# Two batches together in the stationary operand: both convolutions of a conv-plus-scores kernel with 64x128 weights on halves of the PE array, in place of 64x64 weights on quarters

## The chip, the cores and the metric

The kernel runs on one core of one Trainium2 chip. The metric is the device time of one execution in microseconds (us). Three runs of the kernel before took 876.03, 878.07 and 881.8 us; the median is 878.07 us. The profile is of one execution with a span of 872.5 us from its first to its last instruction, on core 0, the only one used.

In what follows PE is the matrix engine (TensorE), PEld its weight loads, DVE VectorE, ACT ScalarE, POOL GpSimd and SP SyncE, which issues most of the DMAs.

## The reference, cut to what matters

Input x is (4, 64, 256, 256) float32: 4 batches, 64 channels, images of 256x256. Layer 0 convolves each channel's image with a 256x256 kernel that is an outer product of two vectors of 256, made by two small sine networks from `z`, and adds `x * bias`. Layer 1 forms, for each batch and channel, the Gram matrix of the image's rows, weighs it, sums each row of it, adds that sum to the row and normalises each channel over batch and image.

```python
# layer 0
k = jnp.einsum('ijk,imk->ijmk', hx, hy)[0]           # outer product for each channel
y = irfft2(rfft2(x, 512) * rfft2(k, 512) / 512)[..., :256, :256]
x = y + x * bias[:, None, None]
# layer 1
scores = jnp.einsum('bpsd,bptd->bpst', x, x) * inv_dim
red = jnp.sum(scores * weights[None], axis=-1, keepdims=True)
y = x + red
mean, var = jnp.mean(y, (0, 2, 3)), jnp.var(y, (0, 2, 3))     # keepdims
out = (y - mean) * lax.rsqrt(var + 1e-5) * gamma + beta
```

As the kernel of layer 0 is an outer product, the 2-D convolution is one along the columns followed by one along the rows, and each is a product with a lower triangular Toeplitz matrix. All arithmetic is float32.

## The kernel before

The kernel takes the 64 channels one after the other. For a channel c the 4 batches are written as two bits (u, v), and 256 rows or columns as 4 blocks of 64. PE has three stages for a channel:

- `conv_z(c, m)` (line 211), m = 0, 1: the convolution along the columns. Weights (`lhsT`) are 64x64 blocks of the image, moving data (`rhs`) are rows of the Toeplitz tile `toep`. A block i of 64 columns reaches only the outputs behind it, so that its moving data has 256 - 64 i columns: 256, 192, 128 and 64. The result lies in a PSUM tile p1 for each u, and `copy_z` (line 220, ACT) copies it to the tile z in SBUF with its columns turned round.
- `conv_x0(c, z)` (line 236; `first_x0`, line 265, for channel 0): the same along the rows, with 64x64 blocks of z as weights. `add_bias` (line 246, DVE) adds `bias * x` on the way from PSUM (p2) to the tile x0 in SBUF.
- `gram(c, v)` (line 299): the blocks of the Gram matrix, 64x64 weights, moving data of 192 and 128 columns. `weigh` (DVE, lines 319 and 328) multiplies with the weights and sums.

The tensor engine's array has 128 rows and 128 columns. A product of 64 rows (its contraction) by 64 columns (of its weights) takes one quarter of it. The row half is given by the partitions of the operands, the column half by the partitions of the output. In the convolutions the four products of one step, t = 0 to 3, go to the four quarters: two bits of the batch are row half and column half. In `conv_z` u is the row half and v the column half, in `conv_x0` it is the other way round.

The order on every engine is written out by hand (`manual_schedule`). In the main loop of channel c, PE runs `conv_x0(c)`, `conv_z(c + 1, 0)`, `conv_z(c + 1, 1)`, `gram(c, 0)`, `gram(c, 1)`, so that ACT's copy of z lies beside other products. SP issues the loads of x for channels c + 2 and c + 3 in four DMAs of 256 KB for a channel, among the loads of `toep`, the weights and the stores of finished channels. PSUM has 8 banks, given out in turn from one pool `ps`. Near the end, in `last_channels`, the row sums of the last three channels are made by PE in place of POOL (`red_by_pe`, lines 379 and 384, weights of 128 rows by 64 columns), and the last channel's moments too (`sum_of`, line 507, weights of 128x128 and moving data of one column). At the start two products with 128x128 weights (line 168) keep PE running while the first Toeplitz tile lands.

The x tiles before: `xts[c, v]` of shape [128, 4, 256], with partition (u, column in its block), then block of columns, then row. The tile z before: [128, 2, 4, 256], with partition (v, row in its block), then u, block of rows, column.

Of the kernel before, what the change touches and what calls it, by code (L numbers as in the profile page):

```python
# [8 lines left out]
F32 = mybir.dt.float32  # L9
AF = mybir.ActivationFunctionType  # L10
ALU = mybir.AluOpType
# [4 lines left out]
B, C, S = 4, 64, 256  # L16
P = 128
# [4 lines left out]
H = P // 2  # L22
# [15 lines left out]
def conv_scores_bn_kernel(  # L38
# [19 lines left out]
    nc = tc.nc  # L58
# [3 lines left out]
    ld = ctx.enter_context(tc.tile_pool(name="ld", bufs=3))  # L62
    wk = ctx.enter_context(tc.tile_pool(name="wk", bufs=2))
    sm = ctx.enter_context(tc.tile_pool(name="sm", bufs=3))

    xts, ws, hs = {}, {}, {}

    def load_xt(c, v, n):
        if not n:
            xts[c, v] = ld.tile([P, 4, S], F32, tag=f"xt{v}", name=f"xt_{c}_{v}", bufs=4)  # L70
        part = bass.ts(n, 2)
        nc.sync.dma_start(xts[c, v][:, part], xT[c, v, :, part])

    PARTS = ((0, 0), (1, 0), (0, 1), (1, 1))

    def load_w(c):
        w = ld.tile([P, 10, H], F32, tag="w", name=f"w_{c}", bufs=2)
        nc.sync.dma_start(w, wl[c])
        ws[c] = w
# [20 lines left out]
    nc.sync.dma_start(decay0_sb, decay0)  # L100
    decay_sb = const.tile([P, S], F32, name="decay_sb")
    nc.sync.dma_start(decay_sb, decay)
    for part in PARTS:
        load_xt(0, *part)
    eye_sb = const.tile([P, P], F32, name="eye_sb")
    nc.sync.dma_start(eye_sb, eye)
    chan_sb = const.tile([P, 3, C], F32, name="chan_sb")
    nc.sync.dma_start(chan_sb.rearrange("p a c -> p (a c)"), chan.to_broadcast([P, 3 * C]))
    load_w(0)
    for part in PARTS:  # L110
        load_xt(1, *part)
    g_sb = const.tile([P, GW], F32, name="g_sb")
    nc.vector.memset(g_sb[:, S:], 0.0)

# [8 lines left out]
    with tc.tile_pool(name="fps", bufs=4, space=PSUM) as fps:  # L123
# [3 lines left out]
        for layer in range(3):  # L127
            for n in range(2):
# [5 lines left out]
                a = wk.tile([P, P], F32, tag="fa", name=f"fa_{layer}_{n}")  # L134
# [3 lines left out]
                k = wk.tile([P, P], F32, tag="fk", name=f"fk_{layer}_{n}")  # L138
# [39 lines left out]
    def load_h(c, n):  # L178


        if not n:
            hs[c] = ld.tile([P, 2, GW], F32, tag="toep", name=f"toep_{c}")
        src = bass.AP(
            g_dram.tensor, g_dram.offset + c * 2 * GW + 16 * n,
            [[4 + C * 2 * GW, COPIES], [1, 4], [1, GW + S]],
        )
        rows = hs[c][bass.ts(n, 16)].rearrange("p a r -> p (a r)")
        nc.sync.dma_start(rows[:, : GW + S], src)

    def copy_h(c):  # L190

        toep = hs[c]
        nc.scalar.copy(toep[H:, :, :S], toep[:H, :, :S])  # L193
# [5 lines left out]
    st8, zs = {}, {}  # L199

    def conv_z(c, m):


        toep = hs[c]
        p1 = [ps.tile([P, 2, S], F32, tag="ps", name=f"p1_{c}_{m}_{u}") for u in range(2)]
        for k in range(2):
            for i in range(4):
                for t in range(4):
                    u, v = t % 2, t // 2
                    rows = bass.ts(u, H)  # L210
                    nc.tensor.matmul(  # L211
                        p1[u][bass.ts(v, H), k, : S - H * i],
                        lhsT=xts[c, v][rows, i, bass.ts(2 * m + k, H)],
                        rhs=toep[rows, 1, H * i : S], start=(i == 0), stop=(i == 3),
                    )
        return p1

    def copy_z(c, m, p1):
        for u in range(2):
            nc.scalar.copy(zs[c][:, u, bass.ts(m, 2), :], p1[u][:, :, ::-1])  # L220

    def conv_x0(c, z, parts=range(2)):


        toep = hs[c]
        if not c:
            first_x0(z)
            return
        for m in parts:
            p2 = [ps.tile([P, 2, S], F32, tag="ps", name=f"p2_{c}_{m}_{v}") for v in range(2)]  # L230
            for i in range(2):
                for k in range(4):
                    for t in range(4):
                        v, u = t % 2, t // 2
                        rows = bass.ts(v, H)
                        nc.tensor.matmul(  # L236
                            p2[v][bass.ts(u, H), i, : S - H * k],
                            lhsT=z[rows, u, k, bass.ts(2 * m + i, H)],
                            rhs=toep[rows, 0, H * k : S], start=(k == 0), stop=(k == 3),
                        )  # L240
            add_bias(c, m, p2)

    def add_bias(c, m, p2):
        for v in range(2):
            part = bass.ts(m, 2)
            nc.vector.scalar_tensor_tensor(  # L246
                st8[c][0][:, v, part], xts[c, v][:, part], chan_sb[:, 0, c : c + 1],
                p2[v][:, :, ::-1], ALU.mult, ALU.add,
            )

    def first_x0(z):

        toep = hs[0]
        p2 = [
            [ps.tile([P, 2, S], F32, tag="ps", name=f"p2_0_{m}_{v}") for v in range(2)]
            for m in range(2)
        ]
        for half in range(2):
            for m in range(2):
                for i in range(2):  # L260
                    for k in range(2 * half, 2 * half + 2):
                        for t in range(4):
                            v, u = t % 2, t // 2
                            rows = bass.ts(v, H)
                            nc.tensor.matmul(  # L265
                                p2[m][v][bass.ts(u, H), i, : S - H * k],
                                lhsT=z[rows, u, k, bass.ts(2 * m + i, H)],
                                rhs=toep[rows, 0, H * k : S],
                                start=(i == 0 and k == 0), stop=(i == 1 and k == 3),
                            )  # L270
                if half:
                    add_bias(0, m, p2[m])

    def begin(c):
        x0 = wk.tile([P, 2, 4, S], F32, tag="x0", name=f"x0_{c}", bufs=5)
        red0 = sm.tile([P, B, 2], F32, tag="red0", name=f"red0_{c}")
        sp = wk.tile([P, B, S], F32, tag="sp", name=f"sp_{c}")
        pr = wk.tile([P, B, S], F32, tag="pr", name=f"pr_{c}")
        rd = wk.tile([P, B, S], F32, tag="rd", name=f"rd_{c}")
        st8[c] = (x0, red0, sp, pr, rd)  # L280
# [129 lines left out]
    def minus_mean(mom):  # L410
        nc.scalar.activation(mom[:, 4:5], mom[:, 2:3], AF.Identity, bias=mom[:, 3:4])  # L411
        nc.scalar.activation(mom[:, 5:6], mom[:, 4:5], AF.Identity, scale=-1.0 / (B * S * S))
# [7 lines left out]
    def sum_squares(c, mom):  # L420
        tot = sm.tile([P, 3], F32, tag="tot", name=f"tot_{c}")
        nc.gpsimd.partition_all_reduce(tot[:, 0:2], mom[:, 6:8], P, RED.add)  # L422
        return tot
# [208 lines left out]

    for n in range(4):
        load_h(1, n)
    for part in PARTS:
        load_xt(2, *part)

    def begin_z(c):  # L640
        zs[c] = wk.tile([P, 2, 4, S], F32, tag="z", name=f"z_{c}")

    begin_z(0)
    for u in range(2):
# [4 lines left out]
    def parts_of(c, place):  # L649

        e, f = c - 4, c - 3
        parts = [[(e, 0, 1)], [(e, 1, 0)], [(e, 1, 1)], [(f, 0, 0)], []]
        if c >= C - 4:
            parts[4] = [(f, 0, 1)]
        if c == C - 3:
            parts[0] = []
            parts[4] += [(f, 1, 0), (f, 1, 1)]
        for i, v, n in parts[place]:
            if i >= 0:
                finish(*fins[i], v, n)  # L660

    for c in range(C - 2):
        p, q, f = c - 1, c - 2, c - 3
        begin(c)
        copy_h(c + 1)
        parts_of(c, 0)
        if c + 2 < C and c:
            load_xt(c + 2, 1, 1)
        load_h(c + 2, 0)
        conv_x0(c, zs.pop(c))  # L670
        if q >= 0:
            minus_mean(moms[q])
            squares(q, moms[q], 0)
        parts_of(c, 1)
        if c + 3 < C:
            load_xt(c + 3, 0, 0)
        load_h(c + 2, 1)
        if q >= 0:
            squares(q, moms[q], 1)
            tot = sum_squares(q, moms[q])  # L680
        if f >= 0:
            fins[f] = (f, *scale_shift(f, moms.pop(f), *scales.pop(f)))
        begin_z(c + 1)
        copy_z(c + 1, 0, conv_z(c + 1, 0))
        parts_of(c, 2)
        load_h(c + 2, 2)
        if c + 3 < C:
            load_xt(c + 3, 1, 0)
        load_w(c + 1)
        load_h(c + 2, 3)  # L690
        copy_z(c + 1, 1, conv_z(c + 1, 1))
        if p >= 0:
            pick_red(p)
        parts_of(c, 3)
        if c + 3 < C:
            load_xt(c + 3, 0, 1)
        if q >= 0:
            scales[q] = root(q, tot)
        if c == C - 3:
            copy_h(c + 2)  # L700
        parts_of(c, 4)
        gram(c, 0)
        if p >= 0:
            moms[p] = add_red(p)
        if c == BY_PE:
            all_sum(c, slice(0, 2))
        gram(c, 1)
        if c < BY_PE:
            all_sum(c)
# [72 lines left out]
```

## Time and profile before

| what | value |
|---|---|
| three runs | 876.03, 878.07, 881.8 us |
| span of the profiled execution | 872.5 us |
| median minus that span | 5.6 us |
| mean granted clock of PE over the span | 0.994 |
| records of products, and of weight loads | 24674 each |
| of these `conv_z`, `conv_x0`, `gram` | 8192, 8192 (8064 at line 236, 128 at line 265), 8192 |
| DMA, share of the 16 engines, one period | 58 to 59%, 195 to 211 GB/s |

The program has half as many products as there are records: a float32 product runs as two passes, each with its own weight load and its own record. So one `conv_z` of a channel has 64 products in the program and 128 records.

How to read it: the shares of busy time are over the span, and a record of a product covers its way through the array as well as the stretch in which it takes in columns, so that records of one quarter overlap each other. What a stage takes is therefore read from where stages begin and end, not from summed durations.

### The profile page before, as it was taken

How to read it: one execution, taken by the hardware profiler on the slowest of the kernel's cores; microseconds unless marked ns; L12 is line 12 of the kernel's file. 1: busy time of each engine (PE TensorE's matmuls, PEld its weight loads, DVE VectorE, ACT ScalarE, POOL GpSimd, SP SyncE). 2: the span in 40 equal slices, each digit the busy share in tenths (PEclk: the TensorE clock that was granted, in tenths of full speed). 3: DMA queues.
4: the chain of work that ended last, by engine and by line, in shares of the span. 5: the costliest groups of instructions: out<-in, count | busy, mean ns of one | idle time of the engine just before them, and what ended most of it. 6: DMA issues, size and time to landing. Idle time of an engine off the chain costs nothing.

```text
span 872.5 us, 55963 instructions
## 1 busy us (share of the span) xinstructions
PE 855.9 (98%) x24674; PEld 836.2 (96%) x24674; DVE 755.9 (87%) x2647; ACT 621.9 (71%) x1218; POOL 427.8 (49%) x194
## 2 busy tenths in 40 slices
PE   7999999999999999999999999999999999999995
PEld 5999999999999999999999999999999999999994
DVE  3588988988988988988998998998998988988996
ACT  2256767767767767777777777777777767767786
POOL 0236546546546546546546546546546546546530
PEclk9999999999999999999999999999999999999997
DMA  6724665565565556565565565655555655565535
GB/s 189 221 77 139 198 209 195 201 211 193 201 210 192 200 196 206 202 207 193 203 208 192 203 206 194 205 200 199 203 201 199 202 203 192 204 210 193 190 141 194
DMA packets 89870, 169.69 MB, mean 194 GB/s; under 512 B 10555, under 2 KB 11740, under 8 KB 89628
## 3 DMA queue, kind: packets, MB, share of 16 engines
q1 hardware_dynamic: 88972, 165.52, 55.6%
q8 instruction: 194, 3.18, 1.6%
q10 hardware_dynamic: 656, 0.59, 0.3%
q14 instruction: 48, 0.39, 0.2%
HBM read 98.18 MB, written 67.76 MB: 190 GB/s over the span
## 4 chain that ended last, share of the span: by engine, by line
PE 97%; DVE 2%; DMA 1%; issue 0%; ACT 0%; DVEq 0%; ACTq 0%
PE p L211 32%; PE g L299 32%; PE p L236 32%; PE p L265 0%; DMA toep<-g_sb 0%; PE ph L132 0%; DVE junk L328 0%; DMA zw_sb<-in_zw 0%; PE rp L379 0%; DVE fa L135 0%; DVE x L516 0%; DVE pr L319 0%; PE rp L384 0%; PE s L507 0%; DVE fa L140 0%
## 5 line engine op out<-in xcount | busy, mean ns | idle before, releaser
L348 POOL PARTITION_ALL_REDUCE rd<-sp x62 | 376.8, 6078 | 182.4 <-DVE sp L340 182.4
L211 PE MATMUL p<-toep,xt 64*64 64x256 f32 (+3 forms) x8192 | 304.0, 296 | 0.9 <-DMA toep<-g_sb 0.9
L299 PE MATMUL g<-x 64*64 64x192 f32 (+1 forms) x8192 | 302.5, 296 | 0.0
L211 PEld LDWEIGHTS p<-toep,xt 64*64 64x64 f32 x8192 | 291.4, 133 | 8.6 <-PE idle L168 1.5
L236 PE MATMUL p<-toep,z 64*64 64x256 f32 (+3 forms) x8064 | 298.3, 296 | 0.0
L236 PEld LDWEIGHTS p<-toep,z 64*64 64x64 f32 x8064 | 289.6, 133 | 6.8 <-issue 0.2
L299 PEld LDWEIGHTS g<-x 64*64 64x64 f32 x8192 | 289.7, 133 | 0.8 <-DVE x L246 0.2
L328 DVE SCALAR_TENSOR_TENSOR junk<-g,w 128x192 f32<-128x192 f32 x512 | 160.9, 351 | 81.1 <-PE g L299 77.7
L462 ACT ACTIVATE o<-x,sh,g 128x512 f32<-128x512 f32 x252 | 203.3, 810 | 3.0
L246 DVE SCALAR_TENSOR_TENSOR x<-xt,chan_sb,p 128x512 f32<-128x512 f32 x256 | 173.8, 739 | 7.6 <-PE p L265 7.2
L220 ACT COPY z<-p 128x512 f32<-128x512 f32 x256 | 134.7, 576 | 22.3 <-PE p L211 22.3
L416 ACT ACTIVATE sq<-x,mom 128x1024 f32<-128x1024 f32 x127 | 145.2, 1143 | 3.3 <-DVE x L405 1.1
L364 DVE SCALAR_TENSOR_TENSOR x<-x,rd 128x1024 f32<-128x1024 f32 x122 | 144.1, 1218 | 0.0
L340 DVE SCALAR_TENSOR_TENSOR sp<-eye_sb,red,pr 128x128 f32<-128x128 f32 x492 | 139.0, 344 | 0.0
L368 POOL PARTITION_ALL_REDUCE mom<-mom x61 | 24.5, 401 | 231.1 <-DVE x L364 227.1
L357 ACT COPY rd<-rd 64x512 f32<-64x512 f32 (+1 forms) x62 | 38.0, 612 | 134.8 <-POOL rd L348 134.7
L319 DVE SCALAR_TENSOR_TENSOR pr<-g,w 128x256 f32<-128x256 f32 x256 | 107.3, 419 | 0.0
L193 ACT COPY toep<-toep 64x512 f32<-64x512 f32 x63 | 38.9, 617 | 32.0 <-DMA toep<-g_dram 26.7
L411 ACT ACTIVATE mom<-mom 128x1 f32<-128x1 f32 x62 | 18.2, 293 | 38.0 <-POOL mom L368 37.1
L328 DVE DVE_READ_ACCUMULATOR junk<-g,w 128x1 f32 x512 | 42.2, 82 | 0.0
L422 POOL PARTITION_ALL_REDUCE tot<-mom x62 | 29.8, 481 | 5.1 <-ACT sq L416 5.1
L416 ACT ACTIVATION_READ_ACCUMULATOR sq<-x,mom 128x1 f32 x127 | 23.7, 186 | 0.0
(84 smaller groups left out, 220.4 us busy)
## 6 DMA issues: line engine op xcount, KB each, us to landing
xt<-in_xT SPq DMA_DIRECT2D x256, 256.0 KB
out<-o SPq DMA_DIRECT2D x256, 256.0 KB
w<-in_wl SPq DMA_DIRECT2D x64, 320.0 KB
toep<-g_dram SPq DMA_DIRECT2D x252, 36.0 KB
g_dram<-g_sb SPq DMA_DIRECT2D x1, 320.0 KB
g_dram<-g_sb ACTq DMA_DIRECT2D x1, 320.0 KB
decay_sb<-in_decay SPq DMA_DIRECT2D x1, 256.0 KB
fw_sb<-in_fw ACTq DMA_DIRECT2D x1, 192.0 KB
```

The lines of the kernel that those rows point to most:

```text
L211: nc.tensor.matmul(p1[u][bass.ts(v, H), k, : S - H * i], lhsT=xts[c, v][rows, i, bass.ts(2 * m + k, H)], rhs=toep[rows, 1, H * i : S], sta ...
L220: nc.scalar.copy(zs[c][:, u, bass.ts(m, 2), :], p1[u][:, :, ::-1])
L236: nc.tensor.matmul(p2[v][bass.ts(u, H), i, : S - H * k], lhsT=z[rows, u, k, bass.ts(2 * m + i, H)], rhs=toep[rows, 0, H * k : S], start=(k ...
L246: nc.vector.scalar_tensor_tensor(st8[c][0][:, v, part], xts[c, v][:, part], chan_sb[:, 0, c : c + 1], p2[v][:, :, ::-1], ALU.mult, ALU.add,)
L299: nc.tensor.matmul(gs[u][bass.ts(h, H), o, :], lhsT=xb[rows, v, i, m, :], rhs=xb[rows, v, i, t, :], start=(i == 0), stop=(i == 3),)
L319: nc.vector.scalar_tensor_tensor(pr[:, b].rearrange("p (t s) -> p t s", s=H), g[:, COL, :], 1.0 / math.sqrt(S), w[:, 6:10, :], ALU.mult, A ...
L328: nc.vector.scalar_tensor_tensor(junk, g[:, part, :], 1.0 / math.sqrt(S), w[:, 3 * n : 3 * n + 3, :], ALU.mult, ALU.mult, accum_out=red0[: ...
L340: nc.vector.scalar_tensor_tensor(sp[:, b, part], eye_sb, red0[:, b, n : n + 1], pr[:, b, part], ALU.mult, ALU.add,)
L348: nc.gpsimd.partition_all_reduce(rd[:, part].rearrange("p b s -> p (b s)"), sp[:, part].rearrange("p b s -> p (b s)"), P, RED.add,)
L364: nc.vector.scalar_tensor_tensor(x0[:, v], x0[:, v], 1.0, rd[:, 2 * v, None, :].to_broadcast([P, 4, S]), ALU.mult, ALU.add, accum_out=mom[ ...
L416: nc.scalar.activation(sq, st8[c][0][:, v], AF.Square, bias=mom[:, 5:6], accum_out=mom[:, 6 + v : 7 + v])
L462: nc.scalar.activation(o, y, AF.Identity, bias=sh, scale=g)
```

## The change

The products of the two column halves of one step are joined: their weights, 64x64 each, are laid side by side in SBUF and become one 64x128 operand, which gives all 128 output partitions at once. The loop over t = 0 to 3 (four quarters) becomes one over u (or v) = 0, 1 (two row halves). The number of products in both convolutions is halved, and each has the moving data it had before (256, 192, 128 or 64 columns). `gram` is not touched: it still has 64x64 weights on quarters.

So that the weights of the two batches are neighbours, x is laid out on the host as [partition (u, column), block of columns, block of rows, v, row], and z in SBUF as [partition (v, row), block of rows, block of columns, u, column]. One tile of x for a channel (`xt`, twice as large) takes the place of two, and its four DMAs are by block of columns; they are as large as before and are issued in the same places, with the same 2 KB for each partition. `copy_z` writes runs of 64 elements with gaps of 64 between them, and `add_bias` reads such runs of x; both work on as many elements as before.

```diff
-    def load_xt(c, v, n):
-        if not n:
-            xts[c, v] = ld.tile([P, 4, S], F32, tag=f"xt{v}", name=f"xt_{c}_{v}", bufs=4)
-        part = bass.ts(n, 2)
-        nc.sync.dma_start(xts[c, v][:, part], xT[c, v, :, part])
+    def load_xt(c, i):
+        if c not in xts:
+            xts[c] = ld.tile([P, 4, 4, 2, H], F32, tag="xt", name=f"xt_{c}", bufs=4)
+        nc.sync.dma_start(xts[c][:, i].rearrange("p k v s -> p (k v s)"), xT[c, :, i])
...
     def conv_z(c, m):
...
-                for t in range(4):
-                    u, v = t % 2, t // 2
+                for u in range(2):
                     rows = bass.ts(u, H)
                     nc.tensor.matmul(
-                        p1[u][bass.ts(v, H), k, : S - H * i],
-                        lhsT=xts[c, v][rows, i, bass.ts(2 * m + k, H)],
+                        p1[u][:, k, : S - H * i],
+                        lhsT=xts[c][rows, i, 2 * m + k],
                         rhs=toep[rows, 1, H * i : S], start=(i == 0), stop=(i == 3),
                     )
...
     def copy_z(c, m, p1):
         for u in range(2):
-            nc.scalar.copy(zs[c][:, u, bass.ts(m, 2), :], p1[u][:, :, ::-1])
+            nc.scalar.copy(
+                zs[c][:, bass.ts(m, 2), :, u],
+                p1[u][:, :, ::-1].rearrange("p k (b s) -> p k b s", s=H),
+            )
...
     def conv_x0(c, z, parts=range(2)):
...
-                    for t in range(4):
-                        v, u = t % 2, t // 2
+                    for v in range(2):
                         rows = bass.ts(v, H)
                         nc.tensor.matmul(
-                            p2[v][bass.ts(u, H), i, : S - H * k],
-                            lhsT=z[rows, u, k, bass.ts(2 * m + i, H)],
+                            p2[v][:, i, : S - H * k],
+                            lhsT=z[rows, k, 2 * m + i],
                             rhs=toep[rows, 0, H * k : S], start=(k == 0), stop=(k == 3),
                         )
...
     def add_bias(c, m, p2):
...
             nc.vector.scalar_tensor_tensor(
-                st8[c][0][:, v, part], xts[c, v][:, part], chan_sb[:, 0, c : c + 1],
-                p2[v][:, :, ::-1], ALU.mult, ALU.add,
+                st8[c][0][:, v, part].rearrange("p i (k s) -> p i k s", s=H),
+                xts[c][:, part, :, v], chan_sb[:, 0, c : c + 1],
+                p2[v][:, :, ::-1].rearrange("p i (k s) -> p i k s", s=H), ALU.mult, ALU.add,
             )
...
     def begin_z(c):
-        zs[c] = wk.tile([P, 2, 4, S], F32, tag="z", name=f"z_{c}")
+        zs[c] = wk.tile([P, 4, 4, 2, H], F32, tag="z", name=f"z_{c}")
...
-    xo = a["x"].reshape(2, 2, C, S, 4, H)
+    xo = a["x"].reshape(2, 2, C, 4, H, 4, H)
...
-        "xT": xo.transpose(2, 1, 0, 5, 4, 3).reshape(C, 2, P, 4, S),
+        "xT": xo.transpose(2, 0, 6, 5, 3, 1, 4).reshape(C, P, 4, 2 * S),
```

`first_x0` is changed as `conv_x0` is, and the calls of `load_xt` name a block i = 0 to 3 in place of a pair (v, n).

More of the change, by code (lines that the diff above doesn't have):

```diff
@@ L66, in conv_scores_bn_kernel @@
     xts, ws, hs = {}, {}, {}
-    def load_xt(c, v, n):
-        if not n:
-            xts[c, v] = ld.tile([P, 4, S], F32, tag=f"xt{v}", name=f"xt_{c}_{v}", bufs=4)
-        part = bass.ts(n, 2)
-        nc.sync.dma_start(xts[c, v][:, part], xT[c, v, :, part])
-    PARTS = ((0, 0), (1, 0), (0, 1), (1, 1))
+    def load_xt(c, i):
+        if c not in xts:
+            xts[c] = ld.tile([P, 4, 4, 2, H], F32, tag="xt", name=f"xt_{c}", bufs=4)
+        nc.sync.dma_start(xts[c][:, i].rearrange("p k v s -> p (k v s)"), xT[c, :, i])
     def load_w(c):
@@ L102, in conv_scores_bn_kernel @@
     nc.sync.dma_start(decay_sb, decay)
-    for part in PARTS:
-        load_xt(0, *part)
+    for i in range(4):
+        load_xt(0, i)
     eye_sb = const.tile([P, P], F32, name="eye_sb")
@@ L109, in conv_scores_bn_kernel @@
     load_w(0)
-    for part in PARTS:
-        load_xt(1, *part)
+    for i in range(4):
+        load_xt(1, i)
     g_sb = const.tile([P, GW], F32, name="g_sb")
@@ L261, in first_x0 @@
                     for k in range(2 * half, 2 * half + 2):
-                        for t in range(4):
-                            v, u = t % 2, t // 2
+                        for v in range(2):
                             rows = bass.ts(v, H)
                             nc.tensor.matmul(
-                                p2[m][v][bass.ts(u, H), i, : S - H * k],
-                                lhsT=z[rows, u, k, bass.ts(2 * m + i, H)],
+                                p2[m][v][:, i, : S - H * k],
+                                lhsT=z[rows, k, 2 * m + i],
                                 rhs=toep[rows, 0, H * k : S],
@@ L634, in conv_scores_bn_kernel @@
         load_h(1, n)
-    for part in PARTS:
-        load_xt(2, *part)
+    for i in range(4):
+        load_xt(2, i)
     def begin_z(c):
-        zs[c] = wk.tile([P, 2, 4, S], F32, tag="z", name=f"z_{c}")
+        zs[c] = wk.tile([P, 4, 4, 2, H], F32, tag="z", name=f"z_{c}")
     begin_z(0)
@@ L667, in conv_scores_bn_kernel @@
         if c + 2 < C and c:
-            load_xt(c + 2, 1, 1)
+            load_xt(c + 2, 3)
         load_h(c + 2, 0)
@@ L675, in conv_scores_bn_kernel @@
         if c + 3 < C:
-            load_xt(c + 3, 0, 0)
+            load_xt(c + 3, 0)
         load_h(c + 2, 1)
@@ L687, in conv_scores_bn_kernel @@
         if c + 3 < C:
-            load_xt(c + 3, 1, 0)
+            load_xt(c + 3, 1)
         load_w(c + 1)
@@ L695, in conv_scores_bn_kernel @@
         if c + 3 < C:
-            load_xt(c + 3, 0, 1)
+            load_xt(c + 3, 2)
         if q >= 0:
```

## The prediction

> **What bounds the kernel now.** First the head of the page, busy times and the chain that ended last:
>
> ```profile
> span 872.5 us, 55963 instructions
> PE 855.9 (98%) x24674; PEld 836.2 (96%) x24674; DVE 755.9 (87%) x2647; ACT 621.9 (71%) x1218; POOL 427.8 (49%) x194
> ...
> PE 97%; DVE 2%; DMA 1%; issue 0%; ACT 0%; DVEq 0%; ACTq 0%
> ```
>
> The end is set by PE. The question is what PE is busy with: taking in moving columns, or loading weights. PEld at 96% warns that the second is not far. The windows of one half period (two stages) and of a whole period in the steady part:
>
> ```profile
> core 0: us, PE busy (x) PEld busy (x) DVE busy (x) ACT busy (x) POOL busy (x), PEclk, DMA share, GB/s
> 404.28:408.65 4.37, 4.37 (x137) 4.27 (x133) 4.29 (x12) 4.37 (x8) 2.62 (x1) 1.00 0.59 197
> 413.08:426.16 13.08, 13.08 (x390) 12.89 (x384) 11.71 (x42) 9.73 (x20) 6.92 (x3) 1.00 0.58 197
> ```
>
> A period is 13.08 us for one channel: three stages (both convolutions and the Gram blocks) of 4.36 us. In the first row PE is in `conv_z` alone; the granted clock is full. Now the products by shape (count, busy us, mean ns of one):
>
> ```profile
> L211 PE MATMUL p<-toep,xt 64*64 64x256 f32 x2048 | 207.2, 377 | 0.9 <-DMA toep<-g_sb 0.9
> L211 PE MATMUL p<-toep,xt 64*64 64x192 f32 x2048 | 179.1, 323 | 0.0
> L211 PE MATMUL p<-toep,xt 64*64 64x128 f32 x2048 | 151.6, 269 | 0.0
> L211 PE MATMUL p<-toep,xt 64*64 64x64 f32 x2048 | 124.8, 217 | 0.0
> ```
>
> Each 64 columns more cost (377 - 217) / 3 = 53.3 ns in one pass; the rest is latency, 217 - 53 = 164 ns, in which the next record runs. So a quarter takes in a pass of 256, 192, 128, 64 columns in 213, 160, 107, 53 ns, 533 ns together. A stage has 128 records, 32 for each quarter, 8 of each width: 8 x 533 ns = 4.27 us. The stage takes 4.36 us; the 0.09 us left are about 3 ns for each of 32 records. So all four quarters stream all the time, and what is loaded is hidden entirely, even behind the narrowest products. The records of single products agree: at 851.42 us, where the quarters are in step, four 64-column products start within 20 ns and the second passes of the same four 56 ns after them.
>
> Last, what a load costs by its columns: the loads in the tail, where 128x128 weights meet one moving column, so that nothing but loading is left.
>
> ```profile
> L211 PEld LDWEIGHTS p<-toep,xt 64*64 64x64 f32 x8192 | 291.4, 133 | 8.6 <-PE idle L168 1.5
> L507 PEld LDWEIGHTS d<-last,each 128*128 128x128 f32 x2 | 0.3, 188 | 2.7 <-DVE x L516 2.7
> 863.68 0.97 PEld L507 LDWEIGHTS s<-last,each 128*128 128x128 f32 x4
> 863.20:864.50 1.30, 1.30 (x8) 1.30 (x7) 0.72 (x4) 1.30 (x2) 0.00 (x0) 0.50 0.00 0
> ```
>
> At full clock a record of 128 columns takes 188 ns against 133 ns for 64: 55 ns for 64 columns. Four loads in a row span 0.97 us at clock 0.50 (fourth row), and one of them lasts 333 ns there; they follow each other by (970 - 333) / 3 = 212 ns, 106 ns at full clock. So a load occupies its part of the array for 106 ns at 128 columns, and by the difference for about 53 ns at 64; the other 80 ns of its record are latency. A 64-column load has the length of a 64-column pass, which is why it hides today.
>
> **The change, part by part.** The sum is made against the profiled execution: 872.5 us span, and 5.6 us between it and the median of the runs.
>
> 1. *Streaming: 0.* Half as many products, each over twice the output columns, two at a time in place of four. Each row half sees 32 records in a stage, as each quarter did, with the same widths. Fewer instructions save nothing, as issue is not the bound: the four products above started 7 ns apart.
>
> 2. *Loads of 128 columns: +54.6 us.* The next load begins some 2 ns after a pass begins (single records), and is hidden if it is done when the pass has been taken in. 256 and 192 columns (213 and 160 ns) cover 106 ns; 128 columns just do (107 ns). 64 columns take 53 ns: the next pass waits 53 ns more. There are 8 such records for each half in a stage: 8 x 53.3 = 0.427 us. Two convolutions of 64 channels make 128 stages: 54.6 us. If the 128-column records lose the 3 ns of slack as well, 128 x 8 x 3 ns = 3 us come on top.
>
> 3. *Changes of the array's division: +21.9 us.* Today all three stages use quarters, and products of one stage start before the last of the other end. With the change `gram` stays on quarters, and each channel goes to halves and back. The trace has no change from 64x64 to 64x128, but the last channels go from 64x64 to 128x64 and back (the chain of waits: start, us, what):
>
> ```profile
> 839.04 0.44 PE rp L384 x8
> 839.48 2.33 PE g L299 x64
> 841.81 2.18 PE p L211 x64
> 843.99 2.18 PE g L299 x64
> 846.17 0.58 PE rp L379 x4
> ```
>
> A half `gram` after such a change takes 2.33 us, one without it 2.18: 0.15 us. The other way, four passes of 256 columns on two column halves need 2 x 216 = 0.43 us and take 0.58: again 0.15. In it lies one 53 ns load that nothing hides; towards halves this load has 128 columns, so 0.20. There are 63 changes in each direction that are new (62 rounds of the main loop and one around the last `conv_z`): 63 x (0.20 + 0.147) = 21.9 us. As both forms keep 64 rows, the price could be nothing; I take 0.147 because the rows that change form in this trace all show it, and keep 0 for the range. Upwards: at a change the slowest quarter sets the end. At 838.0 us the quarters were 0.2 us apart; with every change costing 0.1 us of that, 13 us more. As a change also puts them in step again (the starts after 839.4 us lie within 21 ns), I take 0.
>
> 4. *Copies, bias, DMAs: 0.* `copy_z` (576 ns) and `add_bias` (739 ns) handle the same 512 elements with other strides. DVE has 13.08 - 11.71 = 1.37 us idle in a period and gets some 1.2 more; four `add_bias` would each have to take 0.64 us longer before DVE sets the period. ACT has more room (9.73 of 13.08). If runs of 64 elements cost nothing or double it, PE still sets the end. The four 256 KB loads of x keep their places in SP's queue, two channels ahead of their use, at 58% of the DMA engines; one tile is given free where two were, after the same `add_bias`. No wait is added.
>
> Sum: 872.5 + 54.6 + 21.9 = 949.0 us span, and with 5.6 us around it 954.6: forecast 955 us, 8.7% slower.
>
> A rule that speaks against the change is weighed here. The same-quarter overlap is shown: a half stage has 16 records for each quarter in 2.18 us, 136 ns each, which is streaming (133) alone. The Trainium skill, "TensorE: Matmul & The Clock Gate", Part 3 (The mechanism), says that a weight load overlaps running products only where the row group differs. By that rule each record of the quarters would already cost load plus pass, 186 ns, which the 136 ns refute; for the halves it would make 106 + 136 ns, or 32 x 106 ns = 3.4 us more a stage. The measurement decides here.
>
> The same page, Part 2 (step 1), states that column tiling uses 4 or 8 of the buses that feed the array and row tiling none extra. That fits four loads within one 56 ns step, and says that the change gives such buses up; no run here shows buses.
>
> **Rivals.**
>
> - *The load hides after all.* If a half loads its 128 columns as two 64-column quarters do now, side by side, in 53 ns, part 2 is 0: 872.5 + 21.9 + 5.6 = 900 us. For it: those two loads do run within 56 ns today. Against: the 106 ns of the 128-column rows, which are one instruction as the new loads are. If the change of division is free too, 878 us, no change.
> - *No price for the changes of division,* part 2 as forecast: 878.1 + 54.6 = 933 us.
> - *Faster.* One mechanism: the 3 ns between records belong to four quarters sharing one stream of instructions; with half as many instructions the gap vanishes. Place: between any two records of the convolutions. Price: 128 stages x 0.09 us = 11.5 us, 866.5 us (-1.3%). It decides only if both part 2 and part 3 are below that, so it also needs hidden loads and free changes. Against: the products of lines 379 and 384, on two halves, follow each other after 109 ns for 128 columns, the same 2 to 3 ns.
> - *Loads of the two halves one after the other.* Then each pair of records costs at least 2 x 106 = 213 ns: eight records (four widths, two passes) take 2 x (216 + 3 x 213) = 1710 ns against 1090, a stage 2.5 us more, 128 stages 317 us: 878.1 + 317 + 21.9 = 1217 us. Against: loads of both row halves run within one 56 ns step today. No overlap of load and pass at all would be worse, 128 x 3.4 + 878 + 22, some 1335 us.
>
> **How the numbers follow.** Loads exposed and changes paid, 955 us (940 to 975): 0.66. Loads exposed, changes free, 933: 0.10. Loads hidden, changes paid, 900: 0.07. Both free, 878: 0.05. Faster: 0.03. Serial or unhidden loads, above 1200: 0.09. What a measurement of this kernel can tell from no change is about 1%. Slower by over 1% adds up to 0.66 + 0.10 + 0.07 + 0.09 = 0.92, the same 0.05, faster 0.03. The range for 8 in 10 holds the first three cases: from 897 (just below the 900) to 980 (955, 13 us for quarters out of step, 3 us for 128-column records, and the runs' own spread). The likeliest case alone has 940 to 975.
>
> **What would show it.** PE's records fall to about 16500. The weight loads of lines 211 and 236 have 64x128 and a mean near 188 ns. A convolution stage takes 4.8 us (part 2; 4.37 if the load hides, 6.8 if loads are serial), the period about 14.3 us. Single records: 64-column products follow each other after 109 ns in place of 56. Each stage that changes form begins with 0.15 to 0.2 us of its chain without streaming; `gram` takes 4.36 + 0.15 us. Part 4 is wrong if PE shows waits on DVE, ACT or DMA in the steady part. The forecast is wrong as a whole if 64x128 loads last no longer than 133 ns.

## The result, and the profile after

The changed kernel takes 949.61 us (median of 4 runs, 949.45 to 949.77) against 878.8 us (4 runs, 876.03 to 881.8): a ratio of 1.079, 95% interval 1.075 to 1.083. The profiled run took 949.77 us with a span of 948.0 us; the prediction's sum for the span was 949.0 us.

The head of the page of the changed kernel:

```profile
span 948.0 us, 39454 instructions
PE 932.1 (98%) x16482; PEld 878.3 (93%) x16482; DVE 756.1 (80%) x2647; ACT 636.4 (67%) x1218; POOL 427.5 (45%) x194
```

PE has a third fewer records and is busy 76 us longer. In this kernel `conv_z` is line 207, `conv_x0` line 234, `gram` line 297. One period in its chain of waits (start, us, what):

```profile
401.90 4.51 PE g L297 x128
406.41 4.96 PE p L234 x64
411.37 4.81 PE p L207 x64
```

The period is 14.28 us; it was 13.08. All three stages took 4.36 us before. `conv_z`, which follows a stage of its own form, is 0.45 us longer, `gram` 0.15 us, and `conv_x0`, which begins with the change to halves, 0.60 us. The sum, 1.20 us, times 63 is 75.6 us; the span grew by 75.5. In the steady part PE's products wait for no other engine. Its weight loads have one row of waits that names one (who waited for whom, us in total, times, longest):

```profile
PEld p L234 <- ACT r L428: 10.1, 59, 0.2
```

These are the 0.17 us at each change to halves, and the name is a coincidence: ACT's copies of z, which `conv_x0` reads, ended 3.3 us earlier, and in the run with four changes a period (below) the same idle time before line 234, 10.7 us in 62 times, is put down to no engine ("issue"). So the whole loss is inside PE. Products and loads by shape (count, busy us, mean ns):

```profile
L207 PE MATMUL p<-toep,xt 64*128 64x256 f32 x1024 | 169.1, 404 | 0.1
L207 PE MATMUL p<-toep,xt 64*128 64x192 f32 x1024 | 127.4, 322 | 0.0
L207 PE MATMUL p<-toep,xt 64*128 64x128 f32 x1024 | 100.8, 270 | 0.0
L207 PE MATMUL p<-toep,xt 64*128 64x64 f32 x1024 | 87.8, 245 | 0.0
...
L207 PEld LDWEIGHTS p<-toep,xt 64*128 64x128 f32 x4096 | 302.6, 187 | 12.6 <-PE idle L165 1.2 <-issue 0.2
```

The load's record is 187 ns, 133 before. The 192- and 128-column records last what they did before (323 and 269 ns). Two groups are longer: 245 against 217 ns at 64 columns, and 404 against 377 ns at 256. Single records tell why: in `conv_z` at 400.36 us the first pass of 64 columns has 218 ns and the second 272, the first pass of 256 that follows 432 and its second 376. Each pass that comes behind a 64-column one carries about 55 ns in which it waits for its own weights. The load beside a pass starts about 2 ns after the pass begins to take in columns. The loads beside the two 64-column passes and beside the pass behind them start at 400.364, 400.476 and 400.587 us: 112 and 111 ns apart, where such passes were 56 ns apart before.

### The profile page after: what moved, and what is told of

It is laid out like the page before. It is cut to its first block, busy times and chain, and to the rows that moved or that the text cites. A ratio compares the mean times of both kernels' runs of the same rounds, so it can differ in the third digit from the quotient of the medians.

```text
span 948.0 us, 39454 instructions
## 1 busy us (share of the span) xinstructions
PE 932.1 (98%) x16482; PEld 878.3 (93%) x16482; DVE 756.1 (80%) x2647; ACT 636.4 (67%) x1218; POOL 427.5 (45%) x194
## 4 chain that ended last, share of the span: by engine, by line
PE 97%; DVE 1%; ACT 0%; DMA 0%; issue 0%; DVEq 0%; POOLq 0%; ACTq 0%
PE p L234 33%; PE p L207 33%; PE g L297 30%; PE p L263 1%; PE idle L165 0%; PE ph L129 0%; DVE junk L326 0%; DMA zw_sb<-in_zw 0%; PE rp L377 0%; PE ph L145 0%; DVE fa L132 0%; ACT o L460 0%; DVE pr L317 0%; PE rp L382 0%; ACT sq L414 0%
## 5 line engine op out<-in xcount | busy, mean ns | idle before, releaser
L207 PE MATMUL p<-toep,xt 64*128 64x256 f32 (+3 forms) x4096 | 319.4, 311 | 0.1
L234 PEld LDWEIGHTS p<-toep,z 64*128 64x128 f32 x4032 | 296.8, 187 | 22.1 <-ACT r L428 10.1
L234 PE MATMUL p<-toep,z 64*128 64x256 f32 x4032 | 316.8, 312 | 0.0
L207 PEld LDWEIGHTS p<-toep,xt 64*128 64x128 f32 x4096 | 302.6, 187 | 12.6 <-PE idle L165 1.2
L297 PE MATMUL g<-x 64*64 64x192 f32 (+1 forms) x8192 | 293.2, 297 | 0.0
L297 PEld LDWEIGHTS g<-x 64*64 64x64 f32 x8192 | 267.7, 133 | 14.4 <-DVE u L438 0.2
L216 ACT COPY z<-p 128x512 f32<-128x512 f32 x256 | 137.4, 589 | 70.5 <-PE p L207 66.5
```

The source lines that it names most:

```text
L207: nc.tensor.matmul(p1[u][:, k, : S - H * i], lhsT=xts[c][rows, i, 2 * m + k], rhs=toep[rows, 1, H * i : S], start=(i == 0), stop=(i == 3),)
L216: nc.scalar.copy(zs[c][:, bass.ts(m, 2), :, u], p1[u][:, :, ::-1].rearrange("p k (b s) -> p k b s", s=H),)
L234: nc.tensor.matmul(p2[v][:, i, : S - H * k], lhsT=z[rows, k, 2 * m + i], rhs=toep[rows, 0, H * k : S], start=(k == 0), stop=(k == 3),)
L297: nc.tensor.matmul(gs[u][bass.ts(h, H), o, :], lhsT=xb[rows, v, i, m, :], rhs=xb[rows, v, i, t, :], start=(i == 0), stop=(i == 3),)
```

## Experiments

The theory: half of each period's loss and more is the 128-column load that a 64-column pass can't cover, the rest is the change between quarters and halves twice a period. Rivals: only one of these costs; the price is for the form of the array, not for the load's width; or the new layouts cost. Each run is compared with the kernel before on the same chip: 875.2 us for the first four, 875.3 us for the second four, 881.2 us for the last four.

**Is it the load behind narrow passes?** Three edits of the kernel on halves and one control.

The 64-column products take in 128 columns (in both convolutions and `first_x0`):

```diff
-                        p1[u][:, k, : S - H * i],
+                        p1[u][:, k, : S - H * min(i, 2)],
...
-                        rhs=toep[rows, 1, H * i : S], start=(i == 0), stop=(i == 3),
+                        rhs=toep[rows, 1, H * min(i, 2) : S], start=(i == 0), stop=(i == 3),
```

> The changed kernel with the products of 64 moving columns taking in 128 (the last 128 columns of the Toeplitz tile in place of the last 64), in both convolutions: these products add other values to 64 more outputs, so the convolution is changed there. Theory: the pass of 64 columns already lasts as long as a load of 128 weight columns, so the doubled stream is free: 946 to 951 us. Rival (passes of 64 columns are short, the loss is elsewhere): 8 x 53.3 ns x 128 stages = 54.6 us more, 1004 us.

The same on quarters:

> Control of the same edit in the kernel before (quarters): the products of 64 moving columns take in 128, so the convolution is changed there. Theory: on quarters the pass is bound by its stream and the load of 64 columns hides: 53.3 ns for each of 8 passes of a quarter in 128 stages, 878.8 + 54.6 = 933 us, ratio 1.062. If it stays at 879 us, quarters are bound by something else than the stream, and the theory falls.

Measured: 953.1 us on halves and 925.6 us on quarters. In the convolutions, the narrowest quarter of all products with twice the columns costs 50 us on quarters and 3.5 us on halves. The chains of waits, first of the kernel on quarters, then of the one on halves:

```profile
400.97 4.77 PE p L211 x128
405.75 4.35 PE g L299 x128
410.09 4.77 PE p L236 x128
```

```profile
403.92 4.51 PE g L297 x128
408.43 5.01 PE p L234 x64
413.44 4.81 PE p L207 x64
```

On quarters a convolution stage goes from 4.36 to 4.77 us, 0.41 us where 8 x 53 ns = 0.43 were expected. On halves the period goes from 14.28 to 14.33 us. So a pass of 64 columns does last as long as one of 128 there. The 0.05 us, 3 us in all, put the run just outside the expected interval (951). They lie at a place that the expectation forgot: beside the last pass of `conv_z` lies no 128-column load, as a change of division follows, and there the wider pass shows. From the start of the last product's record to the start of `gram`'s first it is 0.267 us in the changed kernel (401.565 to 401.832) and 0.320 us here (403.530 to 403.850). (In the rows these 0.05 us stand at `conv_x0`, because a piece of the chain runs from the end of one stage's last record to the end of the next stage's last.) So a narrow pass of a 64x128 product is short where no wide load lies beside it, which speaks against the rival that the product's own width makes it long.

The order of the blocks changed, so that the 64-column products lie between wide ones (the same edit in `conv_x0`):

```diff
-            for i in range(4):
+            for i in (0, 3, 1, 2):
...
-                        rhs=toep[rows, 1, H * i : S], start=(i == 0), stop=(i == 3),
+                        rhs=toep[rows, 1, H * i : S], start=(i == 0), stop=(i == 2),
```

> The changed kernel with the blocks of one accumulation in the order 0, 3, 1, 2, so with moving data of 256, 64, 192, 128 columns in place of 256, 192, 128, 64. Theory (each pass waits for the one load that runs beside the pass before it; the longer of the two counts, and their sum does not depend on the order): 949.6 us within 2 us. Rival (loads are made two ahead, or a long pass can pay for the load behind a short one): the 64-column passes now lie between long ones and up to 50 us come back.

On top of it, 96 weight columns for blocks 1 and 3 (the same edit in `conv_x0`):

```diff
+                    cols = 96 if i in (1, 3) else P
                     nc.tensor.matmul(
-                        p1[u][:, k, : S - H * i],
-                        lhsT=xts[c][rows, i, 2 * m + k],
+                        p1[u][:cols, k, : S - H * i],
+                        lhsT=xts[c][rows, i, 2 * m + k].rearrange("p v s -> p (v s)")[:, :cols],
```

> As the run with the order 0, 3, 1, 2, and the products of blocks 3 and 1 with 96 weight columns in place of 128: the last 32 output partitions get nothing from these blocks, which is left out of both convolutions. So both loads that run beside 64-column passes have 96 columns. Theory (a load takes 53 ns for each 64 columns): such a load is 80 ns, the wait behind a 64-column pass falls from 53 to 27 ns, 8 x 26.7 ns x 128 stages = 27.3 us less, 922 us. Rival (the price is for leaving the quarters, whatever the load's width): 949 us.

Measured: 953.8 us and 926.6 us. Nothing comes back from the order; it is 4 us slower than the changed kernel, outside the 2 us expected, with the period of 14.33 us that the padded kernel has, and for the same reason: the last pass of `conv_z` is now one of 128 columns. The narrower loads then take off 27.2 us, expected were 27.3; the 922 us, reckoned from the changed kernel, are missed by the 4 us of the order. The loads and the period of that run:

```profile
L208 PEld LDWEIGHTS p<-toep,xt 64*128 64x128 f32 x2048 | 154.1, 187 | 1.0 <-PE idle L165 0.8 <-issue 0.2
L208 PEld LDWEIGHTS p<-toep,xt 64*96 64x96 f32 x2048 | 129.8, 161 | 17.9
```

```profile
405.36 4.51 PE g L299 x128
409.87 4.80 PE p L236 x64
414.67 4.60 PE p L208 x64
```

133, 161, 187 ns for 64, 96, 128 columns: 27 ns for each 32. Both convolution stages fall by 0.21 us (from 5.01 and 4.81), eight passes by 27 ns, and `gram` stays. The price is the width of the load beside a narrow pass. That a long pass can't pay for the load behind a short one says that one load runs ahead, not two.

**Is it the change of division?** Halves in `conv_x0` alone (`conv_z` with the four quarters t and `lhsT=xts[c][rows, i, 2 * m + k, v]`):

```diff
-                for u in range(2):
+                for t in range(4):
+                    u, v = t % 2, t // 2
                     rows = bass.ts(u, H)
                     nc.tensor.matmul(
-                        p1[u][:, k, : S - H * i],
-                        lhsT=xts[c][rows, i, 2 * m + k],
+                        p1[u][bass.ts(v, H), k, : S - H * i],
+                        lhsT=xts[c][rows, i, 2 * m + k, v],
```

> Halves in conv_x0 alone; conv_z and gram on quarters, new layouts. Changes of division stay as many as in the changed kernel (two a period), exposed loads are halved. Theory: 878.8 + 27.3 (64 stages of 0.427 us) + 21.9 = 928 us, ratio 1.056; 925 us if the last load before each change of division hides in it. Rival A (only loads cost): half of the 75.5 us by which the span grew, 917 us. Rival B (only changes of division cost): all of it, 950 us.

Measured: 921.4 us, 46.1 us above the 875.2 us of the kernel before on that chip; the theory had 46 to 49, rival A 38, rival B 71 to 76. The chain of that run, where line 235 is `conv_x0` and line 208 `conv_z` on quarters, which now begins with a change:

```profile
407.67 4.96 PE p L235 x64
412.62 4.53 PE p L208 x128
417.15 4.35 PE g L298 x128
```

`conv_x0` on halves has the 4.96 us of the changed kernel, `conv_z` pays 0.17 us for the change, and `gram`, which follows a stage on quarters, pays nothing.

`gram(c, 0)` between the two halves of `conv_z`, for four changes a period, on halves and as a control on quarters:

```diff
+        gram(c, 0)
         copy_z(c + 1, 1, conv_z(c + 1, 1))
         if p >= 0:
             pick_red(p)
...
         parts_of(c, 4)
-        gram(c, 0)
```

> The changed kernel with gram(c, 0) put between conv_z(c + 1, 0) and conv_z(c + 1, 1): four changes of division in a period in place of two, the same products. Theory: 62 x (0.20 + 0.147) = 21.5 us more, 971 us; 968 us if the load behind the last 64-column pass hides in the change. Rival (changes are free, all of the loss is loads): 949 us or, with one exposed load less for each change, 946 us.

> Control: the same order in the kernel before, where all stages are on quarters. Theory: no change of division, so no price: 876 to 881 us. If it is slower by over 5 us, the order itself costs (a wait of PE on DVE's bias), and that part must be taken off the run on halves.

Measured: 969.0 us on halves, 19.4 us above the changed kernel and between the 968 and 971 expected, and 877.2 us on quarters, 1.9 us above the kernel before (ratio 1.0023, interval 1.0010 to 1.0036). The trace of that control has four pauses of PE, 2.1 us together, of the kind that the next part explains, so the order itself need not cost anything. The pieces of one period on halves:

```profile
407.67 2.33 PE g L297 x64
410.00 2.55 PE p L207 x32
412.55 2.33 PE g L297 x64
414.89 4.96 PE p L234 x64
419.85 2.41 PE p L207 x32
```

Each half `gram` takes 2.33 us where 2.18 is the length without a change, and the half `conv_z` behind one 2.55 where 2.41 is that without. The new pair of changes costs 0.30 us a period (14.58 against 14.28), 62 times: 18.6 us, which fits the case that the load behind the last 64-column pass hides in the change.

**Do the layouts cost?** The products back on quarters, the new layouts kept:

> The new layouts of X and z with the products back on quarters (64x64 weights, four at a time). Theory (all of the loss is 128-column loads and changes of the array's division): nothing is left of the loss, 876 to 881 us, ratio 1.00, period 13.08 us. Rival (the layout costs: copies with gaps of 64 elements, loads by block of columns): it stays above 1.01; all of it would be 950 us.

Measured: 912.7 us (905.6 to 917.5), ratio 1.044, interval 1.041 to 1.048. The theory missed: undoing the products leaves half of the loss. The chain of that run has something that neither kernel had:

```profile
402.76 4.25 PE p L236 x90
407.01 0.83 issue
407.83 0.34 PE p L236 x6
```

PE stands still in the middle of a stage, waiting for nothing that the profile shows. Places in the steady part where more than 0.28 us lie between the starts of two products: none in the kernel before, 33 here. Of these, 23 come after the 193rd or 194th of PE's records counted modulo 256, and all of those end 1.2 to 1.6 us after a 16 KB packet of the instruction queue (q8 in the page) has landed. Such packets are one for every 256 instructions, 194 in this run as in the kernel before. PE had run out of instructions. Around that place in a block 40 records take 0.81 us on average, 0.68 elsewhere and at the same place in the kernel before; 194 times 0.13 us are some 25 of the 30 us by which this run's span exceeds that of the kernel before on the chip. The other ten pauses stand at the first products of a `conv_z`, where a new `toep` is read for the first time. Why now? The packets of 2 KB, in which x is loaded and results are stored, took 107 ns on average, 93 in the kernel before (99 in a hundred within 0.64 against 0.31 us). Among them the instruction packets start later, in the median 1.5 us after PE enters the block before theirs, 0.7 in the kernel before, while they themselves last 1.0 us in both. The loads of `toep` land late too: ACT waited 91.5 us for them in all, 26.7 in the kernel before. In DRAM the 2 KB pieces of one load lie 8 KB apart in the new layout, 4 KB in the old. Four runs told this apart from the copies and the tiles in SBUF.

The new layouts on quarters with X in DRAM by block of columns first, so that pieces are neighbours:

```diff
-        nc.sync.dma_start(xts[c][:, i].rearrange("p k v s -> p (k v s)"), xT[c, :, i])
+        nc.sync.dma_start(xts[c][:, i].rearrange("p k v s -> p (k v s)"), xT[c, i])
...
-        "xT": xo.transpose(2, 0, 6, 5, 3, 1, 4).reshape(C, P, 4, 2 * S),
+        "xT": xo.transpose(2, 0, 6, 5, 3, 1, 4).reshape(C, P, 4, 2 * S).transpose(0, 2, 1, 3),
```

> The new layouts on quarters again (912.7 us), X with the same tile in SBUF but in DRAM by block of columns first, so that the 2 KB pieces of one DMA lie next to each other; in the run before they are 8 KB apart, in the kernel before 4 KB. Theory (new, from that run's trace: 2 KB packets take 107 ns in place of 93, the packets that bring PE its instructions come later, and PE stalls at every 256th instruction record where one is late): packets of 93 ns or less, no stalls of PE, 875 to 881 us. Rival A (the copies of z with gaps, or the tile of X in SBUF, cost the 37 us): it stays near 912 us.

The kernel before with pieces 8 KB apart:

```diff
-        nc.sync.dma_start(xts[c, v][:, part], xT[c, v, :, part])
+        nc.sync.dma_start(xts[c, v][:, part], xT[c, :, v, part])
...
-        "xT": xo.transpose(2, 1, 0, 5, 4, 3).reshape(C, 2, P, 4, S),
+        "xT": xo.transpose(2, 1, 0, 5, 4, 3).reshape(C, 2, P, 4, S).transpose(0, 2, 1, 3, 4),
```

> The kernel before with one thing changed: in DRAM the pieces of one DMA of X lie 8 KB apart in place of 4 KB; tiles, products and order are those of before. Theory: 2 KB packets near 107 ns, stalls of PE for its instructions, 900 to 915 us. Rival A (tiles in SBUF, copies): 876 to 879 us.

The kernel before with the new z alone (`copy_z` and the tile z as in the change, `lhsT=z[rows, k, 2 * m + i, u]`):

> The kernel before with the new layout of z alone (copies with gaps of 64 elements, products on quarters), X as before in DRAM and in SBUF. Theory: no cost, 875 to 881 us. Rival A (the copies): 900 us or more.

The changed kernel with neighbouring pieces (the edit of the first of these four):

> The changed kernel (halves) with X in DRAM by block of columns first. Theory: on halves PE needs two thirds of the instructions and shows no stall for them, so the faster loads change nothing: 947 to 952 us, and the 2 KB packets fall from 116 to about 93 ns. Rival (late transfers are part of the 75 us): 935 us or less.

Measured, against 881.2 us:

| run | us | ratio, 95% interval | mean 2 KB packet | gaps over 0.28 us, time beyond the usual spacing |
|---|---|---|---|---|
| new layouts on quarters, neighbours | 876.4 | 0.994, 0.992 to 0.997 | 99.5 ns | 6, 2.5 us |
| before, 8 KB apart | 919.0 | 1.042, 1.035 to 1.049 | 111.3 ns | 60, 39.9 us |
| before, new z | 881.4 | 0.999, 0.997 to 1.002 | 98.1 ns | 11, 5.5 us |
| halves, neighbours | 950.5 | 1.077, 1.072 to 1.082 | 98.7 ns | only at changes of division |

The one line of X's layout in DRAM makes the loss in the kernel before and removes it from the new layouts; copies and tiles in SBUF cost nothing. Between the first run and the last, which have the same layouts, only the products differ: 74 us, the price of the joined products by themselves. The waits of PE in the kernel before with pieces 8 KB apart (engine, line, who, us in total, times, longest):

```profile
PE p L236 <- issue: 13.3, 22, 1.3
PE p L211 <- issue: 5.2, 9, 1.2
PE g L299 <- issue: 4.2, 10, 1.0
```

On halves the same change in DRAM does nothing (950.5 against 949.6 us), though its packets fell from 116 to 99 ns: with 130 instruction packets in place of 194, PE doesn't run out. The traces show the room. Counted in the same way, the 194th record of a block in the steady part starts at least 2.7 us after its packet has landed in the changed kernel, in the median 5.1; in the kernel before it is 1.3 and 2.5 us, in the run with new layouts on quarters 1.1 and 1.7, and the pauses all end 1.2 to 1.6 us after a landing. The 93 ns expected of the runs with neighbouring pieces were missed in both, and so was "no stalls" in the first, which has six. The times came out as expected in the first and the last run; the second lost 4 us more, and the third lies 0.4 us above its 881.

The first of these runs is the only one below the kernel before on its own chip, by 0.3 to 0.8%. It is the layouts of the change without its products.

## Why the prediction was right

**What bounds.** Right. Quarters stream all the time: twice the columns in the narrow products cost nearly their full price there (50 of 54.6 us).

**Step 1, streaming 0.** Right for the changed kernel. "Issue is not the bound" was true of the kernel before, but closer than I saw: the quarters use 256 instructions in a stage and get the next ones from DRAM in time, with so little to spare (1.3 us at the least from landing to use, where the pauses end at 1.2 to 1.6) that slower transfers broke it. The view that would have told was in the page (194 instruction packets, one for each stage), and I did not ask when they landed.

**Step 2, loads.** Right in mechanism and size. In single records two terms are off, and by luck they cancel: the passes of 64 and 128 columns come 112 and 111 ns apart where 109 and 110 were reckoned, some 0.06 us a period, and the last pass of `conv_z` hides its load in the change of division, 0.05 us a period back. Per period 2 x 0.427 us was forecast for this step and 0.347 for the next, 1.20 together; 1.20 was measured.

**Step 3, changes of division.** Right: 0.15 us, read from changes to another form (128x64), held for 64x128, where `gram` shows 0.15, and the 0.20 towards halves came out as 0.21 in single records (the first pass of `conv_x0` begins 0.21 us later than a pass within a stage would). Nothing in the trace before assured that the price of one form holds for another; here it did. That quarters out of step would add to it did not happen.

**Step 4, copies, bias and DMAs.** The sum needed 0, and 0 it was, but the reason given, that the loads keep their places in the queue, was incomplete, and that it came out is luck. The packets of the loads became slower, 116 ns against 93, and what covers this is the smaller number of instructions (two thirds of PE's), which I had put down as worth nothing. Without that cover it costs 37 us. So the spans of the changed kernel and the kernel before differ by 75.5 us, but by the medians the changed kernel loses only some 37 us to its own layouts on quarters.

**The sum.** The span was forecast at 949.0 us and was 948.0. The 955 us are 5.4 too high, of which 1.0 is the span and 3.8 lie in the 5.6 us put around it: this was the distance from one profiled execution to the median of other runs, and those scatter by 6 us. In the changed kernel the profiled run has 1.8 us around its span.

**Rivals.** Loads that hide: refuted by the records and by the run with 96 columns. Free changes: refuted by the run with four a period. Serial loads of the two halves: `conv_z` would have taken 6.8 us. Faster by a vanishing gap between records: the gap stayed, 192-column passes (160 ns) follow each other after 162.5 ns. The sentence of "TensorE: Matmul & The Clock Gate" (Part 3, The mechanism) weighed in the prediction, that loads overlap only products of another row group, is refuted on halves too as it stands there: `conv_z` would have needed 32 x 106 ns more than 4.36 us, 7.8 us, and takes 4.81. The same section excepts a load into a background weight buffer; whether that is what happens here no run shows.

## What to carry to other kernels

Compare, product by product, the length of a pass with the length of the weight load beside it: joining two narrow weights into one wide one halves the products but doubles the load, and every pass shorter than the load beside it then costs the difference. A stage that leaves the form of its neighbours pays at both ends; here the price could be read from a place in the trace before where another form already changes. When a layout edit comes along with another, run it alone: here the 37 us that it costs by itself were hidden entirely by the other half of the change.

## What the runs showed of the hardware

- A load occupies a half or quarter of the array for about 27 ns per 32 weight columns of float32 at full clock, one load ahead: 133, 161, 187 ns records for 64, 96, 128 columns, of which by estimate 80 ns (133 - 53) are latency. Loads of the four quarters run side by side: in the kernel before, four start within 20 ns at 851.42 us, in a step of 56 ns.
- A change between quarters and halves costs PE about 0.15 us with a 64-column load behind it (`gram`, 4.51 against 4.36 us) and 0.2 us with a 128-column one (`conv_x0`, 0.21 us).
- PE can run out of instructions without a branch or a wait. The Trainium skill, "Runtime: NRT & Kernel Launch", Instruction fetch mechanics, says that instructions come in blocks of 16 KB, 256 of them, over DMA, and that the fetch is mostly hidden. The block size agrees with the runs (stalls after the same record modulo 256); the hiding doesn't hold on quarters, where PE uses a block every 4.36 us and slower data transfers led to up to 60 gaps, 40 us. The scatter of the kernel before (876 to 889 us beside the last four runs, against 949.45 to 949.77 on halves) may have the same cause: the run with the new z, which is as slow as those, has 11 gaps, 10 of them at this place in a block. The kernel before itself was not traced there.
- Why 2 KB pieces 8 KB apart load more slowly (111 ns a packet in the kernel before when so laid out, 98 at 4 KB in the run with the new z, both on one chip) stays open. Distance alone is not enough: with halves in `conv_x0` only, pieces lie 8 KB apart too, and packets took 93.5 ns. Whether the time in the period at which transfers fall decides it, no run shows.
